# Moving five layer norms of a two-layer hybrid kernel from the scan stage into its last stage

## The chip, the core and the metric

The kernel runs on one core of a Trainium2 chip. The core's engines work side by side, each through its own queue in order: PE (TensorE, matrix products into PSUM), DVE (VectorE), ACT (ScalarE), POOL (GpSimd) and SP (SyncE, which here only starts DMA transfers). POOL starts DMA transfers as well. The metric is the time of one execution on the device in microseconds.

## What is computed

The input `x` is (2, 256, 64, 64): two batches of 256 channels and 4096 positions. Layer 0 is a group norm and a selective scan (Mamba) over the positions, added to `x`. Layer 1 is two of these, forward and backward, behind two layer norms, and then an expert layer on the layer norm of the result. The part that the change touches is the last line:

```python
t = t + _L1_ffn_ref(_ln_t(t), Wr, br, W1, ..., Wo, bo)

def _L1_ffn_ref(x, Wr, br, W1, b1, g1, be1, m1, v1, W2, b2, g2, be2, m2, v2, Wo, bo):
    feat = jnp.mean(x, axis=0)
    w = jax.nn.softmax(feat @ Wr + br, axis=-1)
    h = jnp.einsum('bfd,edh->bfeh', x, W1) + b1
    h = jax.nn.relu(_bn(h, g1, be1, m1, v1))
    h = jnp.einsum('bfeh,ehk->bfek', h, W2) + b2
    h = jax.nn.relu(_bn(h, g2, be2, m2, v2))
    y = jnp.einsum('bfeh,ehd->bfed', h, Wo) + bo
    return jnp.einsum('bfed,fe->bfd', y, w)
```

All eight experts run on every token. The weights `w` of a position are the softmax of logits that are taken from the mean over both batches, so the routes of a position need the norm of both batches there.

## The kernel before

The 4096 positions are cut into 8 chunks of 512 (`T`). A tile of a chunk holds the 256 channels as 2 x 128 partitions, [128, 2, 512] in float32, 512 KB. There are 16 such tiles, one for each batch and chunk, and 128 expert pairs: a pair here is one expert on one batch and chunk.

**The scan stage** runs six jobs one after the other, three for each batch (layer 0, forward, backward), each over 8 chunks. The backward job goes through the chunks from 7 to 0. The main loop (lines 1014 to 1058) walks over half quads, called slots; in each it issues the scans and what a table `sl` has planned for that slot and queue, and `in_order` then fixes the order on every engine. ACT makes the decays (`da`, line 664), POOL the inputs `bq` (line 654) and a part of the products with C (line 715), DVE the scans (line 690) and the rest of the products (line 699), PE the sums over states (line 723) and all projections.

**Features and early experts.** When the backward job has finished a chunk, `finish` (line 744) stores the result in `t_dram` and calls `features` (line 781, called at line 779): mean on PE, subtraction `fcen` on DVE, squares on ACT, variance on PE, the inverse root on ACT, the product on DVE and a store to `nf_dram`. This is the experts' layer norm. The last chunk of the last job is left out (`i + 1 < len(steps)`). A tile that has its features stands in `featured` and in `ready`, and the planner `experts` (line 847) puts its expert pairs into slots of the scan stage as far as its bounds for PE (`PE_ROOM`), ACT (`ACT_ROOM`) and PSUM banks allow; chunks come in the order in which they are ready. Its results `u` go to DRAM (`store`, line 940). It places 80 of the 128 pairs: all of batch 0, and chunks 7 and 6 of batch 1. Those planned beyond the last scan run in a drain (`sl.run_all` at line 1061).

**The last stage** (from line 1065) takes the other 48 pairs: chunks 5, 4, 3, 2, 1, 0 of batch 1. `rest` lists the chunks with pairs left, sorted by the number of early pairs; `whole` lists the two chunks, 7 and 6, that have none left. A pair is `layer` twice (products `hp`, line 1208, and ReLU, line 1212), `weigh` (the product with its route weights `wb`, line 1219, on DVE) and, three pairs later, `last_layer` (products into `y`, line 1227). With it goes side work, one function call at a time:

- the routes of a chunk: `load_n` (POOL starts the loads of the normed tiles, line 1093), `layer_norm` (lines 1095 to 1111, only for a tile without features), `both` (the sum `nm` of both batches on POOL, line 1115), `logits` (PE, line 1122, then six small operations on DVE and one on ACT), `spread` (transposes on PE, line 1147, a store to DRAM, and the load of `wb`, 2 MB, which repeats the weights over the partitions);
- the sums of a chunk: `load_x` (SP), `bias` (PE line 1170, ACT line 1171, and `x` plus bias on POOL, line 1173), `add_early` for each early pair (SP loads `u`, DVE multiplies by `wb`, line 1178, and adds to `x`, line 1179), and `store` (SP, line 1182).

The list `side[i]` holds what goes beside chunk i: first all sums of the whole chunk before, then the routes of the next chunks interleaved with the sums of chunk i. After each pair an equal part of what is left is issued (lines 1289 to 1293). Buffers that matter: `u` has three (the squares of `layer_norm` use the same tag), `n` six, `x` six, `wb` two.

Of the kernel before, what the change touches and what calls it, by code (L numbers as in the profile page):

```python
# [42 lines left out]
F32 = mybir.dt.float32  # L43
# [4 lines left out]
P = 128  # L48
NB, C, L = 2, 256, 4096
KC = C // P  # L50
T = 512
# [24 lines left out]
        out=(16, 18),  # L76
    ),
}
FIRST = -60
E = 8  # L80

# [50 lines left out]
def hybrid_kernel(ctx: ExitStack, tc: tile.TileContext, a: dict, out: bass.AP):  # L132
# [43 lines left out]
    early, u_dram, featured = {}, {}, set()  # L176
# [9 lines left out]
    with ExitStack() as st:  # L186
# [557 lines left out]
        def finish(i):  # L744
            (job, c), ck, tag = steps[i], cks[i], tags[i]
            s, b = job.cols(c), job.batch
            v = {}

            def load():
                v["x"] = wk.tile([P, KC, T], F32, tag="xr", name=f"xr_{tag}")  # L750
                src = t_dram[b] if job.layer else a["x"][b].rearrange("(k p) l -> p k l", p=P)
                nc.sync.dma_start(v["x"], src[:, :, s])

            def over_time(m):
                return v["x"][:, m, ::-1] if job.flip else v["x"][:, m, :]

            def project(m):
                v[m] = psp.tile([P, T], F32, tag="ps", name=f"o_{tag}_{m}")
                nc.tensor.matmul(v[m], ident, over_time(m), start=True, stop=False)
                for j in range(job.nj):  # L760
                    nc.tensor.matmul(  # L761
                        v[m], job.w["out"][:, j, m * P : (m + 1) * P], ck["sz", j],
                        start=False, stop=(j == job.nj - 1),
                    )

            s0 = starts[i + 1]

            before = steps[i - 1][0].nj if i else 0
            sl.put(max(s0 - (10 if job.nj == 4 else 5), starts[i] + (21 if before == 4 else 0)), "sp", load)

            slots = SLOTS[job.nj]["out"] if i + 1 < len(steps) else (3, 4)
            for slot in slots:
                sl.count(s0 + slot, 1 + job.nj, 1, (1,))
            for m, slot in enumerate(slots):
                sl.put(s0 + slot, "pe", lambda m=m: project(m))
                sl.put(s0 + slot + 1, "act", lambda m=m: nc.scalar.copy(over_time(m), v[m]))
            sl.put(s0 + slot + 2, "sp", lambda: nc.sync.dma_start(t_dram[b][:, :, s], v["x"]))
            if job.flip and i + 1 < len(steps):
                features(b, NCH - 1 - c, v, s0 + slot + 2)

        def features(b, c, v, s0):
# [231 lines left out]
        done = []  # L1013
# [51 lines left out]
    with ExitStack() as st:  # L1065
# [17 lines left out]
        def load_n(i):  # L1083

            if (0, i) in n:
                return
            for b in range(NB):
                n[b, i] = mk.tile([P, KC, T], F32, tag="n", name=f"n_{i}{b}", bufs=6)
                if (b, i) in featured:
                    src = nf_dram[b][:, i, :, :]  # L1090
                else:
                    src = t_dram[b][:, :, i * T : (i + 1) * T]
                nc.gpsimd.dma_start(n[b, i], src)

        def layer_norm(i):
            for b in range(NB):
                if (b, i) in featured:
                    continue
                v = n[b, i]
                mean = psp.tile([P, T], F32, tag="ps", name=f"mean_m{i}{b}")  # L1100
                for k in range(KC):
                    nc.tensor.matmul(mean, mean_w, v[:, k, :], start=(k == 0), stop=(k == KC - 1))
                nc.vector.tensor_tensor(v, v, over_channels(mean), ALU.subtract)
                sq = mk.tile([P, KC, T], F32, tag="u", name=f"sq_{i}{b}", bufs=3)
                nc.scalar.activation(sq, v, AF.Square)
                var = psp.tile([P, T], F32, tag="ps", name=f"var_m{i}{b}")
                for k in range(KC):
                    nc.tensor.matmul(var, mean_w, sq[:, k, :], start=(k == 0), stop=(k == KC - 1))
                r = mk.tile([P, T], F32, tag="r", name=f"r_{i}{b}", bufs=1)
                rsqrt(r, var, eps5)  # L1110
                nc.vector.tensor_tensor(v, v, over_channels(r), ALU.mult)

        def both(i):
            n["sum", i] = mk.tile([P, KC, T], F32, tag="nm", name=f"nm_{i}", bufs=1)
            nc.gpsimd.tensor_tensor(n["sum", i], n[0, i], n[1, i], ALU.add)

        def logits(i):

            lt = psp.tile([P, q, E], F32, tag="ps", name=f"lt_{i}")
            for t in range(q):  # L1120
                for k in range(KC):
                    nc.tensor.matmul(
                        lt[:, t, :], n["sum", i][:, k, t * P : (t + 1) * P], wr[:, k, :],
                        start=(k == 0), stop=(k == KC - 1),
                    )
            w = n["w", i] = mk.tile([P, q, E], F32, tag="w", name=f"w_{i}")
            nc.vector.tensor_tensor(
                w, lt, br.rearrange("p (o e) -> p o e", o=1).to_broadcast([P, q, E]), ALU.add
            )
            mx = mk.tile([P, q], F32, tag="mx", name=f"mx_{i}")  # L1130
            nc.vector.tensor_reduce(mx, w, AX.X, ALU.max)

            def over_experts(v):
                return v.rearrange("p (q o) -> p q o", o=1).to_broadcast([P, q, E])

            nc.vector.tensor_tensor(w, w, over_experts(mx), ALU.subtract)
            nc.scalar.activation(w, w, AF.Exp)
            sm = mk.tile([P, q], F32, tag="sm", name=f"sm_{i}")
            nc.vector.tensor_reduce(sm, w, AX.X, ALU.add)
            nc.vector.reciprocal(sm, sm)  # L1140
            nc.vector.tensor_tensor(w, w, over_experts(sm), ALU.mult)

        def spread(i):

            pt = psp.tile([P, T], F32, tag="ps", name=f"wt_{i}")
            for t in range(q):
                nc.tensor.transpose(pt[:E, t * P : (t + 1) * P], n["w", i][:, t, :], ident)
            wts[i] = mk.tile([E, T], F32, tag="wt", name=f"wts_{i}", bufs=3)
            nc.scalar.copy(wts[i], pt[:E, :])
            w_dram = drp.tile([E, T], F32, name=f"w_dram{i}")  # L1150
            nc.gpsimd.dma_start(w_dram, wts[i])
            wb[i] = mk.tile([P, E, T], F32, tag="wb", name=f"wb_{i}")
            nc.gpsimd.dma_start(
                wb[i], w_dram.rearrange("e (o t) -> o e t", o=1).to_broadcast([P, E, T])
            )

        def routes(i):
            return [lambda: load_n(i), lambda: layer_norm(i), lambda: both(i), lambda: logits(i), lambda: spread(i)]

        def load_x(i):  # L1160
            for b in range(NB):
# [76 lines left out]
            (b, i, e) for i in rest  # L1238
            for e in (order if i == rest[0] else range(E)) for b in range(NB) if e >= first[b, i]
        ]  # L1240
        side = {i: [] for i in rest}
        for at, i in enumerate(rest):
            after = rest[at + 1 : at + 2]
            now, work = sums(i), side[i]
            if at:
                for j in whole[at - 1 : at]:
                    work += sums(j)
            ahead = []
            for j in whole[at : at + 1] + after:
                ahead += routes(j)  # L1250
            every = max(1, len(now) // max(1, len(ahead)))
            while now or ahead:
                work += ahead[:1] + now[:every]
                ahead, now = ahead[1:], now[every:]

        load_n(rest[0])
        for name, e in [("W1", order[0]), ("W2", order[0]), ("W1", order[1]), ("W2", order[1])]:
            load_w(name, e)
        nc.sync.dma_start(bo, a["bo"])
        layer_norm(rest[0])  # L1260
        both(rest[0])
        for i in whole[:1] + rest[1:2]:
# [9 lines left out]
        for at, (b, i, e) in enumerate(pairs):  # L1272
            for name, k in weights[: 6 if at else 4]:
                load_w(name, k)
            weights = weights[6 if at else 4 :]
            h = layer(n[b, i], 0, e, f"{i}_{e}_{b}")
            h = layer(h, 1, e, f"{i}_{e}_{b}")
            if at == 0:
                logits(i)
            elif at == 1:  # L1280
                spread(i)

            for p in {0: [], 1: [], 2: waiting[:1], 3: waiting[1:]}.get(at, waiting[-1:]):
                weigh(*p)
            waiting.append((b, i, e, h))
            if len(waiting) > 3:
                last_layer(*waiting.pop(0))
            done[i] += 1
            work = side[i] if at > 1 else []
            upto = -(-len(work) // (count[i] - done[i] + 1))  # L1290
            for fn in work[:upto]:
                fn()
            side[i] = side[i][upto:]
        weigh(*waiting[-1])
        for p in waiting:
            last_layer(*p)
# [104 lines left out]
```

## Time and profile before

| what | us |
|---|---|
| median of three runs (5131.54 to 5132.48) | 5132.12 |
| the profiled execution | 5134.52 |
| its span, first to last instruction | 5132.7 |
| scan stage, end of the last scan's work on DVE | 4507.9 |
| last product of an early expert on PE | 4529.94 |
| first product of the last stage on PE | 4543.67 |
| end of the last product on PE | 5127.16 |

Busy time over the whole span: PE 4283.0 us (83%), DVE 4581.7 (89%), ACT 3681.3 (72%), POOL 4410.3 (86%). These are averages over two stages with different limits. In the page's row of 40 slices DVE and POOL stand at 9 tenths through nearly all of the scan stage and fall to 3 to 6 and to 1 or 0 in the last slices, where PE stands at 8 or 9. So each stage is to be read by itself.

The profile's rows have the form: start, duration, engine, line, operation, output and inputs with the kernel's names, and in brackets the idle time before it with what ended it. "PEld" is the load of a matrix into the array, which overlaps PE. A queue with a small q (SPq) means the sequencer that issues. A matrix product of the program in float32 shows as two passes.

### The profile page before, as it was taken

To read this page: it belongs to the slowest core of one execution; us is meant where nothing else is said; L and a number is where in the kernel's file an instruction comes from. 1 tells how busy PE (TensorE), PEld (TensorE's weight loads), DVE (VectorE), ACT (ScalarE), POOL (GpSimd) and SP (SyncE) were. 2 spreads that over 40 slices of the span, in tenths; PEclk is the share of its full clock that TensorE was granted. 3 is DMA by queue.
4 is the path that set the end of the run, shared out by engine and by line. 5 is a ranking of instruction groups with operands and counts; after the bars stand their busy time and mean duration, and the time that the engine had idled before them with its cause. 6 is when DMAs were issued, how large, how long until landed. Compare 5 with 4: busy or idle time off the path is not lost.

```text
span 5132.7 us, 47350 instructions
## 1 busy us (share of the span) xinstructions
PE 4283.0 (83%) x14920; PEld 1485.7 (29%) x14920; DVE 4581.7 (89%) x3088; ACT 3681.3 (72%) x7474; POOL 4410.3 (86%) x1442
## 2 busy tenths in 40 slices
PE   5677767776668988888988888899999999888999
PEld 1222222221122323333322233233333333333444
DVE  6998999999999999999989999999999999936543
ACT  5777677777767888888888788888778878832232
POOL 5998999999999999999989999999999999911100
PEclk8888888887888999999999999999999999999999
DMA  5454433344444454546654555455554444455532
GB/s 178 149 176 158 164 136 128 132 146 144 151 139 156 170 195 163 184 165 209 207 185 170 174 181 179 159 167 177 195 187 166 167 165 161 168 180 182 191 108 77
DMA packets 321355, 845.49 MB, mean 165 GB/s; under 512 B 35720, under 2 KB 107152, under 8 KB 279120
## 3 DMA queue, kind: packets, MB, share of 16 engines
q1 hardware_dynamic: 316816, 815.07, 46.2%
q0 software_dynamic: 4288, 27.40, 1.4%
q8 instruction: 118, 1.93, 0.2%
q14 instruction: 133, 1.09, 0.1%
HBM read 655.05 MB, written 187.30 MB: 164 GB/s over the span
## 4 chain that ended last, share of the span: by engine, by line
DVE 20%; PE 15%; ACT 10%; issue 4%; POOL 3%; DMA 2%; SPq 0%; DVEq 0%; POOLq 0%; ACTq 0%
DVE da L690 9%; PE hp L1208 5%; DVE bq L699 5%; ACT da L664 4%; PE y L1227 2%; PE e L912 2%; DVE bq L690 2%; POOL bq L654 2%; PE conv L452 1%; POOL bq L715 1%; PE y L723 1%; ACT bq L675 1%; DVE x L1179 1%; DVE u L1178 1%; ACT eh L923 1%
## 5 line engine op out<-in xcount | busy, mean ns | idle before, releaser
L654 POOL TENSOR_TENSOR bq<-rxdt,bc 128x2048 f32<-128x2048 f32 x640 | 2893.2, 4543 | 28.7 <-issue 12.3
L664 ACT ACTIVATE da<-rdt,w_a 128x512 f32<-128x512 f32 x2560 | 1756.8, 686 | 105.4 <-DVE bq L690 59.8
L690 DVE TENSOR_TENSOR_SCAN da<-da,h_state,bq 128x1024 f32<-128x1024 f32 x664 | 1559.1, 2348 | 50.5 <-ACT da L664 34.4
L715 POOL TENSOR_TENSOR bq<-bq,bc 128x2048 f32<-128x2048 f32 (+1 forms) x280 | 1179.9, 4214 | 22.5
L690 DVE TENSOR_TENSOR_SCAN bq<-da,h_state,bq 128x1024 f32<-128x1024 f32 x456 | 1059.3, 2338 | 28.5 <-ACT da L664 28.4
L723 PE MATMUL y<-bq,stack 128*32 128x512 f32 x5120 | 759.4, 687 | 317.4 <-POOL bq L715 297.3
L699 DVE TENSOR_TENSOR bq<-da,bc 128x1024 f32<-128x1024 f32 x760 | 926.5, 1219 | 16.0
L912 PE MATMUL e<-eh,ew 128*128 128x512 f32 x1280 | 626.1, 620 | 66.0 <-DVE sp L513 15.0
L709 ACT COPY h_state<-da 128x2 f32<-128x2 f32 x759 | 119.1, 157 | 641.3 <-DVE bq L699 639.4
L675 ACT ACTIVATE bq<-h_state,bq,a 128x1 f32<-128x1 f32 x1120 | 430.5, 384 | 0.6
L723 PEld LDWEIGHTS y<-bq,stack 128*32 128x32 f32 x5120 | 143.6, 119 | 876.7 <-POOL bq L715 404.9
L1212 ACT ACTIVATE h<-hp,of,sc 128x512 f32<-128x512 f32 x192 | 149.1, 777 | 298.9 <-PE hp L1208 281.7
L912 PEld LDWEIGHTS e<-eh,ew 128*128 128x128 f32 x1280 | 230.3, 193 | 452.0 <-issue 219.4
L414 PE MATMUL xs<-nx,w_in 128*128 128x512 f32 x640 | 318.7, 628 | 40.9 <-DVE xc L466 20.8
L452 PE MATMUL conv<-xs,w_conv 64*64 64x512 f32 x2560 | 332.6, 613 | 21.9 <-ACT xs L436 18.9
L414 PE MATMUL z<-nx,w_in 128*128 128x512 f32 x640 | 323.8, 639 | 18.7 <-DVE sp L513 10.6
L912 PE MATMUL e<-en,ew 128*128 128x512 f32 x640 | 308.3, 613 | 23.9 <-DVE fcen L809 7.8
L761 PE MATMUL o<-sz,w_out 128*128 128x512 f32 x640 | 301.7, 612 | 0.0
L923 ACT ACTIVATE eh<-e,of,sc 128x512 f32<-128x512 f32 x320 | 242.1, 768 | 36.7 <-PE e L912 36.2
L517 POOL TENSOR_TENSOR xdt<-sp,xc 128x512 f32<-128x512 f32 x160 | 203.2, 1273 | 49.9 <-DVE sp L513 49.8
L730 PE MATMUL y<-xc,w_d 128*128 128x512 f32 x320 | 193.1, 688 | 54.2 <-DVE sz L742 53.9
L690 DVE TENSOR_TENSOR_SCAN da<-da,bq 128x1024 f32<-128x1024 f32 x96 | 219.4, 2286 | 6.5 <-ACT da L664 3.6
(139 smaller groups left out, 4940.5 us busy)
## 6 DMA issues: line engine op xcount, KB each, us to landing
rxdt<-xdtd SPq DMA_DIRECT2D x160, 1024.0 KB, 6.8
rdt<-dtd SPq DMA_DIRECT2D x160, 1024.0 KB, 6.5
bc<-bcd SPq DMA_DIRECT2D x384, 256.0 KB, 3.2
dtd<-sp SPq DMA_DIRECT2D x160, 256.0 KB, 3.5
xdtd<-xdt SPq DMA_DIRECT2D x160, 256.0 KB, 4.0
ew<-in_W SPq DMA_DIRECT2D x160, 256.0 KB, 4.3
u<-u SPq DMA_DIRECT2D x80, 512.0 KB, 4.4
u<-eu SPq DMA_DIRECT2D x76, 512.0 KB, 4.0
```

What stands on the lines that cost most here:

```text
L414: nc.tensor.matmul(ps, job.w["in", half][:, k, j * P : (j + 1) * P], rhs, start=(k == 0), stop=(k == KC - 1),)
L452: nc.tensor.matmul(v[r][64 * col : 64 * col + 64, :], job.w["conv"][rows, 2 * jp + j, k, :], ck["xs", jp][rows, j, k : k + T] if k < 4 els ...
L654: nc.gpsimd.tensor_tensor(bq[g], ck["rxdt", j], over_groups(ck["bc", 0, sg]), ALU.mult)
L664: nc.scalar.activation(da[g, h][:, k, :], cks[i]["rdt", j][:, q, :], AF.Exp, scale=steps[i][0].w["a"][:, j, q * SG + sg : q * SG + sg + 1],)
L675: nc.scalar.activation(bq[g][:, q, 0:1], job.h[:, j, sg, q : q + 1], AF.Identity, scale=cks[i]["a0", j][:, h, sg : sg + 1], bias=bq[g][:, ...
L690: nc.vector.tensor_tensor_scan(b if on_pool(g, h) else d, d, b, job.h[:, j, sg, 2 * h : 2 * h + 1] if c else 0.0, ALU.mult, ALU.add,)
L699: nc.vector.tensor_tensor(bq[g][:, two, :], d, cks[i]["bc", 1, sg].rearrange("p (o t) -> p o t", o=1).to_broadcast([P, 2, T]), ALU.mult,)
L715: nc.gpsimd.tensor_tensor(b, b, cks[i]["bc", 1, sg].rearrange("p (o t) -> p o t", o=1).to_broadcast([P, groups, T]), ALU.mult,)
L723: nc.tensor.matmul(y[i, j][q * CG : (q + 1) * CG, :], stack, bq[g][:, q, :], start=False, stop=(sg == SG - 1),)
L761: nc.tensor.matmul(v[m], job.w["out"][:, j, m * P : (m + 1) * P], ck["sz", j], start=False, stop=(j == job.nj - 1),)
L912: nc.tensor.matmul(ps, ew[l][:, k, m * P : (m + 1) * P], key[x][:, k, :], start=(k == 0), stop=(k == KC - 1),)
L923: nc.scalar.activation(key[dst][:, m, :], key["ps", l, m], AF.Relu, bias=of[:, l, e, m : m + 1], scale=sc[:, l, e, m : m + 1],)
```

## The change

Five tiles of batch 1, those of chunks 4, 3, 2, 1 and 0, no longer get their features in the scan stage: `AHEAD = 3` lets only the first three chunks of the last job have them. (Chunk 0 had none before either.) Their norm is made in the last stage. There the norm is cut in two functions: `centred` (mean, subtraction, squares) and `layer_norm` (variance, inverse root, product), which are two entries in the list of routes; the squares have a tag and a buffer of their own.

With four feature norms fewer, the planner places 82 pairs early: experts 0 and 1 of batch 1's chunk 5 come in addition. Since chunk 5 then has more early pairs than the others, `rest` becomes 4, 3, 2, 1, 0, 5. Chunk 4 is the first, and both halves of its norm are issued ahead of the first pair.

The side work now has fixed places. Every entry has a share of the chunk's pairs, and is issued as soon as the share of pairs done is greater: the six parts of the routes at 0, 0.15, 0.25, 0.4, 0.6 and 0.8 (a second chunk's 0.1 later each), and the sums evenly from 0.1 on, those of the whole chunk before first.

```diff
+AHEAD = 3
...
-            if job.flip and i + 1 < len(steps):
+
+            if job.flip and (b < NB - 1 or c < AHEAD):
                 features(b, NCH - 1 - c, v, s0 + slot + 2)
...
-        def layer_norm(i):
+        def centred(i):
             for b in range(NB):
                 if (b, i) in featured:
                     continue
...
                 nc.vector.tensor_tensor(v, v, over_channels(mean), ALU.subtract)
-                sq = mk.tile([P, KC, T], F32, tag="u", name=f"sq_{i}{b}", bufs=3)
+                sq = n["sq", b, i] = mk.tile([P, KC, T], F32, tag="sq", name=f"sq_{i}{b}", bufs=1)
                 nc.scalar.activation(sq, v, AF.Square)
+
+        def layer_norm(i):
+            for b in range(NB):
+                if (b, i) in featured:
+                    continue
+                v, sq = n[b, i], n["sq", b, i]
                 var = psp.tile([P, T], F32, tag="ps", name=f"var_m{i}{b}")
...
-            return [lambda: load_n(i), lambda: layer_norm(i), lambda: both(i), lambda: logits(i), lambda: spread(i)]
+            return [lambda: load_n(i), lambda: centred(i), lambda: layer_norm(i), lambda: both(i), lambda: logits(i), lambda: spread(i)]
...
-        side = {i: [] for i in rest}
+        side = {}
         for at, i in enumerate(rest):
-            after = rest[at + 1 : at + 2]
-            now, work = sums(i), side[i]
+            side[i] = []
+            for k, j in enumerate(whole[at : at + 1] + rest[at + 1 : at + 2]):
+                for part, fn in zip((0, 0.15, 0.25, 0.4, 0.6, 0.8), routes(j)):
+                    side[i].append((part + 0.1 * k, fn))
+            now = sums(i)
             if at:
-                for j in whole[at - 1 : at]:
-                    work += sums(j)
-            ahead = []
-            for j in whole[at : at + 1] + after:
-                ahead += routes(j)
-            every = max(1, len(now) // max(1, len(ahead)))
-            while now or ahead:
-                work += ahead[:1] + now[:every]
-                ahead, now = ahead[1:], now[every:]
+                now = [fn for j in whole[at - 1 : at] for fn in sums(j)] + now
+            side[i] += [(0.1 + 0.9 * k / len(now), fn) for k, fn in enumerate(now)]
+            side[i].sort(key=lambda work: work[0])
...
         nc.sync.dma_start(bo, a["bo"])
+        centred(rest[0])
         layer_norm(rest[0])
         both(rest[0])
...
-            work = side[i] if at > 1 else []
-            upto = -(-len(work) // (count[i] - done[i] + 1))
-            for fn in work[:upto]:
-                fn()
-            side[i] = side[i][upto:]
+            while at > 1 and side[i] and (done[i] == count[i] or side[i][0][0] < done[i] / count[i]):
+                side[i].pop(0)[1]()
```

## The prediction, made before the changed kernel was run

> **What bounds the kernel now.** I read four views in this order: the busy times by window, the chain of waits over the last 600 us, the timeline at the seam between the scans and the experts' stage, and the timeline around the one norm that the last stage already holds.
>
> The windows are cut at the chunks of the last job's scans (the first product of line 730 of each chunk), then at the first expert product of each chunk in the last stage. Columns: length, then busy time of PE, PEld, DVE, ACT and POOL.
>
> ```profile
> 3643.60:3752.60 109.00, 102.36 (x373) 35.89 (x372) 103.09 (x67) 83.63 (x160) 108.44 (x35) 0.97 0.53 185
> 3972.00:4082.50 110.50, 99.97 (x366) 34.95 (x365) 107.03 (x70) 88.56 (x186) 107.39 (x35) 0.97 0.51 175
> 4191.90:4302.60 110.70, 99.96 (x366) 33.88 (x365) 106.98 (x70) 88.93 (x186) 107.43 (x35) 0.95 0.50 169
> ...
> 4507.20:4543.70 36.50, 22.77 (x53) 9.58 (x53) 0.68 (x1) 6.62 (x10) 2.35 (x5) 0.87 0.38 134
> 4628.90:4741.90 113.00, 97.25 (x242) 43.61 (x241) 70.29 (x65) 28.74 (x40) 19.17 (x14) 0.92 0.55 198
> 4741.90:4844.30 102.40, 97.23 (x223) 42.25 (x222) 74.11 (x65) 27.79 (x38) 14.72 (x9) 0.93 0.56 195
> 4844.30:4933.20 88.90, 88.82 (x218) 38.49 (x217) 35.15 (x35) 27.42 (x37) 11.41 (x11) 1.00 0.40 143
> ```
>
> To see: in the scans DVE and POOL are both at 97% and more, and the first chunk shown, which holds no feature norm, is 1.5 us shorter than the other two: there POOL alone is full. In the last stage PE is the bound where nothing goes wrong (88.82 of 88.90), and the second and third chunk lose time. The chain of waits names the cause:
>
> ```profile
> 4693.13 1.15 DVE u L1178
> 4694.30 1.24 DVE x L1179
> 4695.99 5.06 DMA x<-t_dram
> 4701.19 1.18 POOL x L1173
> 4703.49 2.33 POOL x L1173
> 4705.82 3.29 POOL nm L1115
> 4709.15 3.59 PE lt L1122 x16
> ```
>
> The sums of a whole chunk come as one block on DVE; SP's next load stands behind the store of that block, POOL's sum `nm` behind that load, PE's logits behind `nm`: 12.4 us of idle PE. Seam and norm:
>
> ```profile
> 4530.85 0.53 POOL L942 DMA_DIRECT2D u<-eu  x1 [6.61 <-ACT eu L921]
> 4543.67 5.75 PE L1208 MATMUL hp<-n,W 128*128 128x512 f32 x8 [13.73 <-DMA W<-in_W]
> ...
> 4956.37 1.98 PE L1102 MATMUL mean_m<-n,mean_w 128*128 128x512 f32 x4
> 4958.39 1.22 DVE L1103 TENSOR_TENSOR n<-n,mean_m 128x1024 f32<-128x1024 f32 x1 [15.80 <-PE mean_m L1102]
> 4959.65 1.06 ACT L1105 ACTIVATE sq<-n 128x1024 f32<-128x1024 f32 x1 [2.58 <-DVE n L1103]
> 4960.76 3.68 PE L1108 MATMUL var_m<-sq,mean_w 128*128 128x512 f32 x4 [2.40 <-ACT sq L1105]
> 4964.48 0.69 ACT L179 ACTIVATE r<-var_m,columns 128x512 f32<-128x512 f32 x1 [2.47 <-PE var_m L1108]
> 4965.18 1.28 ACT L180 ACT_TABLE_LOAD   x1
> 4966.48 0.63 ACT L180 ACTIVATE r<-r 128x512 f32<-128x512 f32 x1
> ```
>
> To see: the stage starts 13.73 us after the last early expert, on DMA; and a norm with nothing between its steps makes PE idle 2.4 us and then run four passes in 3.68 instead of 1.98 us.
>
> **What the Trainium skill says.** "SBUF — State Buffer", section "SBUF: two separate sides": DVE with two SBUF inputs and POOL hold one shared port pair exclusively. The trace agrees: three `h` products took 6.42 us (2.14 each, else 1.22) beside `nm`, which took 3.32 us instead of 2.34; the subtraction from PSUM at 4958.39 took 1.22 us beside POOL. "TensorE: Matmul & The Clock Gate", "What's actually happening": an idle window of about 3.4 us puts the array at half clock. Here 2.4 us were enough, costing 1.7 us. "ScalarE: Activation LUTs", "What ACT_TABLE_LOAD costs": 1283 ns and a drain of 1380 ns; the trace has 1.28 us and the next activation 0.02 us later, so I use 1.28.
>
> **The change, part by part.** Each Matmult of the program is two passes of 0.43 us (eight passes, 3.43 us in the chain), so an expert pair of 12 costs PE 10.57 us (spacing of `hp` starts in clean pairs).
>
> (1) Scans. The features of four chunks leave: per chunk 4 products, 2 DVE passes of 1.2 us (line 809: 1.21), 4 short ACT passes, a store on SP. By the changed order each of these chunks gets 4 early-expert products for them, so PE stays. DVE loses 2.4 us per chunk. POOL's own floor is some 107.3 us plus 0.6 idle. The chunk without features took 109.0 against 110.3 for the mean of four with them and 36 expert products (110.5, 110.5, 109.4, 110.7): I take 1.5 us x 4 = -6. Bounds: 0 (POOL is the whole limit, or PE) and -9.7 (all DVE time counts).
>
> (2) Drain. After the last scan's sum PE has 38 products instead of 26 ahead of the seam, nothing else runs: 12 x 0.87 = +10.4. The two new pairs 5/0 and 5/1 of the second batch end there; their store gates the seam as pair 6/7's did.
>
> (3) Seam. Chunk 4 becomes first, because chunk 5 has two early pairs; its second-batch tile comes from `t_dram` rather than `nf_dram`. The same source took 9.1 us against 8.4 (medians to landing in the stretch 4900 to 4960): +0.5. Bounds 0 and 1.
>
> (4) First norm, exposed: mean on a cold array 3.7, subtraction 1.25, square 1.1, variance 3.7, logarithm 0.7, table 1.3, exponential 0.65, product 1.3, between them 0.1: +13.8. No pair can hide it, since all need that tile or come later in PE's queue. Bounds 12 and 15.
>
> (5) Pairs: 46 instead of 48, 2 x 10.57 = -21.1.
>
> (6) Norms beside pairs: four instead of one, each 8 passes: 3 x 3.86 = +11.6.
>
> (7) Stalls. Before: 48 x 10.57, 8 logits of 1.70, 8 transposes of 0.44, 8 biases of 1.92 and a norm of 3.86 make 543.7; from 4543.67 to 5127.16 are 583.5, so 39.8 stall. After, worked out from the order:
> - 2.1 cold start, as before.
> - Chunk 3's two halves run in one turn (fractions 0.25 and 0.35, both under 3/8): mean and variance stand together on PE. Ahead of the subtraction DVE waits for `wb` of chunk 4, 12.5 us after its transposes ended (wts copy, 3.5 and 7.5 us to landing); PE is ready 11 us after them. With the slowed product (2.1), subtraction and square the variance is 6.0 late, and cold: 7.7. Bounds 5 and 10.
> - Chunk 2's halves stand together too. Ahead of the subtraction DVE has four of chunk 7's sums, which start 5.05 us after the bias product (4754.32 to 4759.34) and share the port with two POOL passes. Some 15 us from there to the square, PE ready after 9 (one pair less the bias): 6.6 and the cold clock, 8.3. Bounds 4 and 12.
> - Chunk 1's halves are a pair apart, so only its mean can be late: the load of its tile on POOL stands behind the load of `wb` of chunk 2, which waits until DVE has finished with chunk 3. I put the landing 5 us after PE wants it: 6.8 with the cold clock. Bounds 0 and 12.
> - Chunk 0's halves are apart, its loads early: nothing. Table loads sit under PE's products as at 4960.72; with the rest I allow 1.5.
> Together 26.4, so -13.4. The old 12.4 us stall goes because `nm` of chunks 7, 6, 3, 2 and 1 now stands ahead of the late bias sums on POOL.
>
> Steps that cost nothing: the extra 512 KB buffer frees `u`; `mean`, `var` and the table loads on ACT find PE's next products running (ACT is busy 28 of 102 us there); the 10 sums of chunk 5 have six pairs to hide in. If DVE is late, none of this cover holds.
>
> Sum: -6 + 10.4 + 0.5 + 13.8 - 21.1 + 11.6 - 13.4 = -4.2. The profiled execution took 5134.5 with a span of 5132.7, 2.4 over the median of the runs; the difference applied to the median gives 5127.9.
>
> **Rivals.** (A) Forecast: 5127.9, chance 0.42.
> (B) Faster: the norms hide better. Scans give 9 instead of 6, chunk 1's tile is in time (-6.8), chunk 2's subtraction is 2 us earlier: -16 in all, 5116. For it: DVE runs ahead in clean chunks (35 of 89 us busy). Against it: chunks 3 and 2 each carry 24 sums of 2.39 us, 9 products and 5 or 6 POOL passes on the shared port, about 100 us with the waits behind stores. Chance 0.27.
> (C) Scans give nothing, since POOL is their limit: +1.8, 5133.9. For it: POOL 107.4 in every chunk; against it the 109.0 us chunk. Chance 0.10.
> (D) Slower: DVE becomes the bound of chunks 3 and 2. Each store of a finished chunk holds up SP's next loads: before, 5.34, 6.97, 7.03 and 5.87 us of idle DVE, and 13.9 at 4747 where the loads met that of `wb` (I used 5.3 and 7). In the new order loads and a `wb` may meet at two seams; with 13.9 at both, DVE is 13.8 us later. Its logits of chunk 1 have only some 3.5 us before PE's transposes want them: beyond that point each microsecond stalls PE. 10 us there, 3 each at the norms of chunks 3 and 2: +16, so +11.8 and 5143.9. For it: DVE and PE need nearly the same time in these chunks. Against it: each PE stall also gives DVE time back. Chance 0.21.
>
> **How the numbers follow.** About 0.2% (10.3 us) is what a measurement tells from no change. A and C lie within it: 0.52; B is faster: 0.27; D slower: 0.21. B and D at their own values need most of the range: 5114 to 5144 leaves some 2 in 10 outside. A alone spans 5121 to 5136.
>
> **What would show it.** Step 1: chunks 4 to 6 of the last job at 108.5 to 109.5 us. Steps 2 to 4: the first `hp` some 29 us later relative to the last scan. Step 7: gaps of 6 us before `var_m` of chunks 3 and 2, a wait of `mean_m` of chunk 1 for a DMA, none before `lt`. I am wrong if PE waits at `wt` or `lt` for DVE or POOL (D), if `mean_m` of chunk 1 does not wait (B), or if the norm ahead of the first pair is hidden.

## The result, and the profile after

The changed kernel takes 5153.83 us (median of 6 runs, 5151.49 to 5155.26) beside 5131.83 us before (5128.81 to 5133.11): a ratio of 1.0043, 95% interval 1.0033 to 1.0053. It is slower by 22 us. The profiled execution took 5155.26 us with a span of 5153.4, 20.7 more than the span before.

Busy times by window, kernel after. The columns are those of the table in the prediction; the numbers after the last parentheses are the mean granted clock of PE, the DMA share and the DMA's GB/s. The first row is the scans of the last job's last four chunks, the second runs from the last scan's sum on PE to the start of the experts' stage, the third is the first norm, the others are the second to fourth chunk of the last stage.

```profile
4081.00:4494.60 413.60, 382.77 (x1370) 133.96 (x1368) 399.63 (x249) 333.84 (x692) 400.79 (x128) 0.97 0.49 168
...
4494.60:4544.00 49.40, 34.79 (x77) 14.84 (x77) 0.69 (x1) 10.90 (x16) 2.84 (x5) 0.85 0.37 122
4544.00:4558.10 14.10, 7.57 (x9) 2.35 (x9) 2.44 (x2) 4.94 (x5) 0.01 (x1) 0.50 1.07 360
4654.10:4777.10 123.00, 105.62 (x250) 45.71 (x249) 77.97 (x70) 33.46 (x45) 20.09 (x14) 0.89 0.47 163
4777.10:4891.00 113.90, 97.35 (x230) 41.59 (x229) 71.95 (x63) 33.08 (x44) 16.28 (x13) 0.93 0.54 194
4891.00:4983.40 92.40, 92.33 (x225) 39.89 (x224) 39.90 (x38) 31.46 (x41) 9.13 (x7) 1.00 0.37 130
```

The same four chunks before, in the same view:

```profile
4082.50:4507.20 424.70, 386.57 (x1378) 136.96 (x1377) 408.71 (x258) 340.65 (x704) 401.00 (x128) 0.97 0.48 164
```

The scans gained 11.1 us. POOL did the same work (401.00 and 400.79 us), DVE 9.1 us less, ACT 6.8 and PE 3.8 less. So the stretch got shorter by 2 us more than DVE lost, with POOL busy 94% of it before and 97% after. Counted between the first products of line 731, the three chunks that were to take 108.5 to 109.5 us took 107.3, 109.1 and 105.8. In the last stage the chunk without a whole chunk's sums (last row) is as tight as before, 92.33 busy of 92.40. The second and third chunk lose: 123.0 and 113.9 us, with 17 us of idle PE each and a clock of 0.89 and 0.93.

What PE waits for from 4530 us to the end, kernel after. The numbers are us in total, times, longest.

```profile
PE hp L1216 <- ACT h L1220: 26.0, 2, 16.5
PE var_m L1116 <- ACT sq L1107: 14.9, 3, 7.8
PE mean_m L1104 <- DMA n<-t_dram: 14.6, 1, 14.6
PE hp L1216 <- DVE n L1119: 4.0, 1, 4.0
```

The last two rows and 2.6 us of the second are the seam and the first norm, 4.5 and 7.8 of the second row the norms of chunks 3 and 2. The seam and the three norms were forecast. The first row was not: the second layer of a pair waits twice for the ReLU of its first layer, a step of 0.8 us on an engine that is busy 33 of 114 us there. The timeline at the longer of the two, on PE, DVE and ACT:

```profile
4835.56 1.85 PE L1130 MATMUL lt<-wr,nm 128*128 128x8 f32 x16
...
4837.26 3.68 PE L1216 MATMUL hp<-n,W 128*128 128x512 f32 x8
...
4837.84 1.23 DVE L1186 TENSOR_TENSOR u<-u,wb 128x1024 f32<-128x1024 f32 x1 [4.16 <-DMA u<-u]
...
4854.67 1.23 DVE L1187 TENSOR_TENSOR x<-x,u 128x1024 f32<-128x1024 f32 x1
4855.81 0.18 DVE L1135 TENSOR_TENSOR w<-lt,br 128x32 f32<-128x32 f32 x1
4856.03 0.19 DVE L1139 TENSOR_REDUCE mx<-w 128x4 f32<-128x32 f32 x1
4856.25 0.19 DVE L1144 TENSOR_TENSOR w<-w,mx 128x32 f32<-128x32 f32 x1
4856.48 0.23 ACT L1145 ACTIVATE w<-w 128x32 f32<-128x32 f32 x1 [23.37 <-DVE w L1144]
4856.61 1.43 ACT L1220 ACTIVATE h<-hp,of,sc 128x512 f32<-128x512 f32 x2
...
4857.43 6.65 PE L1216 MATMUL hp<-h,W 128*128 128x512 f32 x8 [16.48 <-ACT h L1220]
```

PE has the logits `lt` ready at 4837.4. DVE reaches them at 4855.8, because fourteen operations of whole-chunk sums and one `h` product (1.2 us each) stand before them in its queue. The exponential of the logits (L1145) is ACT's and was issued with the logits, so it stands in ACT's queue ahead of the next pair's ReLUs and holds them for 16 to 17 us; PE stands still and then runs eight products in 6.65 instead of 3.87 us, which the same eight take elsewhere in this kernel. The other stop, 9.5 us, is behind the logits of chunk 6, beside chunk 3. "Perfetto Trace Analysis", section "Tensor Engine Instruction (MATMUL, LD_WEIGHTS)", of the Trainium skill says that ACT and DVE are strictly first in, first out. The trace agrees: two ReLUs whose products had ended by 4840.9 start 0.13 us after that exponential starts. DVE is late without being full: in the second chunk's 123.0 us it is busy 78.0, and ahead of the first stop it waits there 13.9 us for `wb`, 11.7 for POOL's sum of `x` and bias, and 8.1 for loads of `u`.

### The profile page after: what moved, and what is told of

It reads as the page before. It is cut to its first block, busy times and chain, and to the rows that moved or that the text cites. A ratio compares the mean times of both kernels' runs of the same rounds, so it can differ in the third digit from the quotient of the medians.

```text
span 5153.4 us, 47366 instructions
## 1 busy us (share of the span) xinstructions
PE 4285.9 (83%) x14920; PEld 1483.4 (29%) x14920; DVE 4591.5 (89%) x3090; ACT 3691.3 (72%) x7480; POOL 4411.4 (86%) x1443
## 4 chain that ended last, share of the span: by engine, by line
DVE 25%; PE 19%; ACT 12%; POOL 6%; issue 6%; DMA 2%; SPq 0%; DVEq 0%; POOLq 0%; ACTq 0%
DVE da L691 12%; DVE bq L700 6%; ACT da L665 5%; PE hp L1216 5%; POOL bq L655 4%; PE e L914 3%; DVE bq L691 3%; PE y L1235 3%; POOL bq L716 2%; PE conv L453 2%; PE y L724 2%; ACT bq L676 1%; PE o L762 1%; ACT eh L925 1%; DMA dtd<-sp 1%
## 5 line engine op out<-in xcount | busy, mean ns | idle before, releaser
L914 PE MATMUL e<-eh,ew 128*128 128x512 f32 x1312 | 641.2, 620 | 56.4 <-DVE sp L514 14.1
L453 PE MATMUL conv<-xs,w_conv 64*64 64x512 f32 x2560 | 331.3, 610 | 20.9 <-ACT xs L437 19.0
```

The lines of the kernel that those rows point to most:

```text
L453: nc.tensor.matmul(v[r][64 * col : 64 * col + 64, :], job.w["conv"][rows, 2 * jp + j, k, :], ck["xs", jp][rows, j, k : k + T] if k < 4 els ...
L914: nc.tensor.matmul(ps, ew[l][:, k, m * P : (m + 1) * P], key[x][:, k, :], start=(k == 0), stop=(k == KC - 1),)
```

## The experiments

The theory: **the queue**. DVE runs late on the sums of a whole chunk; an ACT operation that needs DVE's result then stands in ACT's queue ahead of ReLUs that do not need it, and PE stops. The rivals: the moved norms themselves take the time, or DVE and the port it shares with POOL are full, so that a wait that is taken away comes back elsewhere. Whether quicker loads of `u` would also have kept DVE in time was not tried. Each median is set against the runs of the kernel before in the same comparison.

**Only the fixed shares.** The norms stay in the scan stage, 80 early pairs, the new side work.

```diff
-AHEAD = 3
+AHEAD = 7
```

> The features back in the scan stage (AHEAD = 7, so 80 early pairs, first chunk 5, one norm left in the last stage), with the fixed shares kept. Theory Q (queue): the vector queue runs late on the sums of chunks 7 and 6, the exponential of the logits waits for it in ACT's queue, and the ReLUs behind it stop PE. The two whole chunks' sums are then beside chunks 4 and 3 just as they are beside 3 and 2 in the changed kernel, so two waits of hp for ACT of 8 to 17 us stay, no others over 3 us: 5120 to 5135 us. Theory N (norms): the five norms in the last stage make the loss and make DVE late; without them the waits go and the fixed shares show their gain over before, whose last stage holds some 36 us of stalls: 5095 to 5110 us.

Measured: 5145.78 us, ratio 1.0025 (1.0015 to 1.0036). PE's waits in the last stage:

```profile
PE hp L1216 <- ACT h L1220: 42.6, 2, 21.8
PE hp L1216 <- DMA n<-nf_dram: 12.6, 1, 12.6
```

With no norm moved, the wait for the ReLU is there, and longer than in the changed kernel. The fixed shares alone cost some 13 us. The time is above both expected ranges: the two waits were 21.8 and 20.9 us where the theory of the queue had 8 to 17.

**Only the moved norms.** `AHEAD = 3`, the old distribution of the side work:

```diff
-                for part, fn in zip((0, 0.15, 0.25, 0.4, 0.6, 0.8), routes(j)):
-                    side[i].append((part + 0.1 * k, fn))
...
+            every = max(1, len(now) // max(1, len(ahead)))
+            while now or ahead:
+                work += ahead[:1] + now[:every]
```

> The norms in the last stage as in the changed kernel, but the side work spread as before (sums of the whole chunk as a block first, then routes and sums interleaved). Theory Q: as the block came first before too, DVE is late again when the logits come; PE waits behind ACT or at POOL's nm for 20 to 40 us, and each norm has its halves in the same turn or the next; 5150 to 5175 us. Theory N: the loss is the norms, the distribution does not matter: within 5 us of the changed kernel, 5149 to 5159 us. If the fixed shares are the loss (theory S), this kernel is at 5120 to 5130 us, as the scan stage's gain of 12 us remains.

Measured: 5161.89 us, ratio 1.0055 (1.0040 to 1.0070), the slowest of all. There is no long wait for a ReLU. PE waits 16.3 us for squares, 10.0 for `nm` on POOL before the logits, 7.5 before the transposes, 5.4 for a tile. So the norms and the fixed shares are not two costs to be added: alone they cost some 29 and 13 us, together 22.

**The exponential one pair later.** The logits' function is cut behind DVE's subtraction of the maximum, and its rest (`soft`: exponential, sum, reciprocal, product) becomes a part of its own. Nothing else moves.

```diff
+        def soft(i):
+            w = n["w", i]
...
-                for part, fn in zip((0, 0.15, 0.25, 0.4, 0.6, 0.8), routes(j)):
+                for part, fn in zip((0, 0.15, 0.25, 0.4, 0.6, 0.7, 0.8), routes(j)):
```

> The changed kernel with the logits cut in two: products, bias, maximum and subtraction where they were, the exponential on ACT and what follows on DVE at a share 0.1 later (one pair). The same work on every engine. Theory Q: the waits of 9.5 and 16.5 us of hp for ACT fall by one pair's time of 10.6 us each, to 0 and about 6, and the cold passes behind the first go: 5153.8 - 20 - 3 = 5131 us, range 5126 to 5138. Rival L (load): DVE and the shared port are the bound of these chunks, so the wait comes back at the transposes wt or at the next norm, and the time stays at 5147 to 5155 us.

Measured: 5133.66 us, ratio 1.0003 (0.9995 to 1.0012), 20.2 us under the changed kernel. PE's waits:

```profile
PE var_m L1116 <- ACT sq L1107: 14.9, 3, 7.8
PE mean_m L1104 <- DMA Wo<-in_Wo: 14.3, 1, 14.3
PE mean_m L1104 <- DMA n<-t_dram: 9.4, 1, 9.4
PE hp L1223 <- DVE n L1119: 4.0, 1, 4.0
PE hp L1223 <- DVE w L1135: 2.4, 1, 2.4
PE hp L1223 <- ACT h L1227: 0.4, 1, 0.4
```

The 26.0 us are gone, the rows of squares are untouched, and the wait for the tile of chunk 1, which the prediction had priced at 6.8 and the changed kernel did not show, appears with 9.4: PE had simply been too late to meet it. So the place in the queue of one operation of 0.23 us, with three small ones of DVE that follow it, is worth 20 us. That shows the queue as the cause of the 26.0 us. Of DVE's lateness a wait of 2.4 us for `lt` is left.

**The other whole chunk's sums later.** Chunk 6's sums go from beside chunk 2 to beside chunk 1, and its routes from beside chunk 3 to beside chunk 2; the exponential stays early.

```diff
-            for k, j in enumerate(whole[at : at + 1] + rest[at + 1 : at + 2]):
+            for k, j in enumerate((whole[at // 2 : at // 2 + 1] if at % 2 == 0 else []) + rest[at + 1 : at + 2]):
...
-            if at:
-                now = [fn for j in whole[at - 1 : at] for fn in sums(j)] + now
+            if at % 2:
+                now = [fn for j in whole[at // 2 : at // 2 + 1] for fn in sums(j)] + now
```

> The changed kernel with the routes of chunk 6 beside chunk 2 and its 16 sums beside chunk 1 instead of chunk 2. Theories Q and L: chunk 2 then has 8 sums instead of 24, DVE is in time for its logits and the wait of 16.5 us with its 2.8 us of cold passes goes; beside chunk 1 DVE is late in turn, as a chunk with 24 sums, and one wait of 5 to 17 us appears there at the logits of chunk 0. Time 5140 to 5154 us. If the lateness came from the norm of chunk 1 standing in DVE's queue ahead of the sums (theory N), the chunk without sums loses nothing and chunk 1, whose norm partner is chunk 0, loses as much: no change, 5150 to 5156, and the same wait moves with the norm. A wait at the logits of chunk 3's second route (9.5 us) stays under both.

Measured: 5149.55 us, ratio 1.0034 (1.0021 to 1.0048); the intervals overlap with those of the changed kernel. PE's waits for ReLUs:

```profile
PE hp L1216 <- ACT h L1220: 33.4, 2, 16.8
```

A wait stays in chunk 3, now behind the logits of chunk 2 and longer than expected (16.6 us, 9.5 in the changed kernel), and the other moves with the sums to chunk 1 (16.8 us at 4945.7). One whole chunk beside one chunk is enough to make DVE late; two in a row aren't needed.

**Seven norms ahead and the late exponential**, the edits of the first and third run together:

```diff
-AHEAD = 3
+AHEAD = 7
```

> Features back in the scan stage (AHEAD = 7) together with the late exponential of x_exp_late; with x_ahead7, x_exp_late and the changed kernel it makes a square. Theory Q: the two waits of 21.8 and 20.9 us lose 10.6 us each, and some more where DVE no longer waits for ACT: 5145.8 - 22 = 5124 us (5119 to 5129), so the norms' move costs some 8 to 10 us with either order of the exponential (5153.8 - 5145.8 = 8; 5133.7 - 5124 = 10). Theory N (norms make DVE late, and the exponential only shows it): the move costs nothing once the exponential is late, 5130 to 5137 us.

Measured: 5124.48 us, ratio 0.9982 (0.9975 to 0.9989). The ReLU's wait is gone, and PE waits 21.6 us in another way:

```profile
PE hp L1223 <- DVE w L1135: 21.6, 2, 13.3
```

DVE's lateness now reaches PE through PSUM, where `hp` and `lt` share one set of buffers: a product of the first layer needs one that still holds logits which DVE has not read, and starts 0.24 us after DVE starts to read them. The four runs make a square: moving the norms costs 8.0 us with the early exponential (5153.8 against 5145.8) and 9.2 with the late one (5133.7 against 5124.5).

**Three repairs of the norms**, each on top of the one before, the late exponential in all: the norm's second half a pair after the first; then chunk 5, which has its features, as first chunk of the stage, so that no norm stands ahead of it; then a third buffer for `wb`.

```diff
-                for part, fn in zip((0, 0.15, 0.25, 0.4, 0.6, 0.7, 0.8), routes(j)):
+                for part, fn in zip((0, 0.15, 0.3, 0.4, 0.6, 0.7, 0.8), routes(j)):
...
-        rest.sort(key=lambda i: sum(first[b, i] for b in range(NB)))
+        rest.sort(key=lambda i: (any((b, i) not in featured for b in range(NB)), sum(first[b, i] for b in range(NB))))
...
-            wb[i] = mk.tile([P, E, T], F32, tag="wb", name=f"wb_{i}")
+            wb[i] = mk.tile([P, E, T], F32, tag="wb", name=f"wb_{i}", bufs=3)
```

> x_exp_late with the second half of a norm at share 0.3 instead of 0.25, so that a pair stands between the halves for chunks 3 and 2 as well. The waits of var_m of 4.5 and 7.8 us and 1.8 us of cold passes at each go: -15 of waits if nothing takes their place, 5119 us. Theory L (DVE is the bound of chunks 3 and 2): the variance is in time, but DVE gets no more time, and the wait is passed on to the logits' exponential or to the tile of chunk 1, which already makes PE wait 9.4 us: 5125 to 5134 us. I expect half of it to be passed on: 5126 us.

> x_apart with chunk 5 first again (six pairs, its tiles have features), so that chunk 4's norm is beside pairs. The norm ahead of the first pair, 14.1 us from the first mean product to the first hp, goes from PE's idle time: -10.2 (14.1 less 3.9 of work that stays) against x_apart if its halves are hidden. Rival: chunk 5 has only six pairs to hide the routes of 7 and 4 and its 10 sums, so DVE or POOL's loads are late by the first pairs of chunk 4: gain below 4 us.

> x_first5 with three buffers for wb instead of two. POOL then need not wait for DVE's last product of a chunk before it loads the next wb and the tiles behind it in its queue. If the 9.4 us wait of mean_m for a tile from t_dram is due to that block, it goes, with 1.8 us of cold passes: -8 to -11 us against x_first5. If it is due to the transfers all running at once, or to the n buffers, it stays: within 3 us.

Measured: 5129.90 (ratio 0.9995, 0.9986 to 1.0004), 5131.89 (0.9999, 0.9990 to 1.0007) and 5124.60 us (0.9983, 0.9975 to 0.9992). The first takes away the 12.3 us at the norms of chunks 3 and 2, and 6.8 us for ReLUs and 4.8 for the logits' buffer come back (0.4 and 2.4 before it). The second takes away the first norm's exposed chain, and a wait of 11.4 us for the squares of chunk 4 takes its place, since nothing of the side work is issued before the stage's third pair, so that both halves of that norm fall into one turn there while DVE waits for `wb`: a miss. Neither of the two is told apart from the run with the late exponential (the intervals overlap). The third is 9.1 us below that run; it takes away the late tile of chunk 1 (7.2 us in the run before it): the load of that tile stands on POOL's queue behind a `wb` load which waits for a buffer, as step 7 had said.

**The whole chunks' sums spread.** On top of the late exponential, the norm's second half at 0.3 and chunk 5 first: half of chunk 7's sums goes beside each of the second and third chunks, half of chunk 6's beside each of the fourth and fifth, with a buffer of their own for their weights and other shares for the routes beside the first chunk; then the same with seven norms ahead.

```diff
+            for j in whole[(at - 1) // 2 : (at - 1) // 2 + 1] if at else []:
+                of_j = sums_of.setdefault(j, sums(j))
+                now += of_j[:11] if at % 2 else of_j[11:]
+            now += sums(i)
```

> The changed kernel with the logits' exponential one pair later, the last job's featured chunk 5 first in the last stage, the second half of a norm at 0.3 of a chunk's products, and the sums of the two whole chunks no longer each beside one chunk: half of chunk 7's sums beside each of the second and third chunks of the stage, half of chunk 6's beside each of the fourth and fifth, with a buffer of their own for the whole chunks' weights. Theory (VectorE is late only because a whole chunk's sums fall beside one chunk, and every wait left in the stage follows from that lateness): the waits of the same kernel with whole sums and three buffers, 11.1 us (chunk 4's norm), 5.1 (the ReLU) and 8.8 (a logits buffer not read), go, and with them some 5 us of products that restart slowly: 5124.6 - 25 - 5 = about 5095, taken as 5093 to 5106. Rival (VectorE and the port that it shares with GpSimd are full in the whole stage, so that evened work only moves the waits): 5118 to 5128, with waits of over 15 us in all spread over more chunks.

> The same as the run with evened sums, but with the norms of all seven chunks ahead of the last stage, as in the kernel before, and the exponential one pair later. Theory of lateness: the two waits of 8.3 and 13.3 us for a logits buffer in the run with seven norms ahead and the late exponential go, some 3 us of slow restarts with them: 5124.5 - 24.6 = about 5100, taken as 5096 to 5107. If moving the norms costs some 8 to 9 us on top in every variant, as in the two pairs of runs so far, this is 8 us under the run with three norms ahead; if evened sums give VectorE room for the norms, the two lie within 4 us. Rival (VectorE full): 5118 to 5128.

Measured: 5110.36 us (ratio 0.9962, 0.9947 to 0.9977) and 5107.23 us (0.9951, 0.9934 to 0.9968). From 4600 us on PE is busy throughout in both but for 1.5 us, so DVE isn't full: it was late only where a whole chunk's sums fell beside one chunk. The first kernel misses its expected range by some 4 us (the second by 0.2), for a wait of 13.4 us at the beginning of the stage:

```profile
4572.36 1.98 PE L1104 MATMUL mean_m<-n,mean_w 128*128 128x512 f32 x4
...
4576.92 1.95 DVE L1235 TENSOR_TENSOR h<-h,wb 128x1024 f32<-128x1024 f32 x1 [19.47 <-DMA wb<-w_dram]
...
4588.19 1.21 DVE L1105 TENSOR_TENSOR n<-n,mean_m 128x1024 f32<-128x1024 f32 x1
...
4589.43 1.06 ACT L1107 ACTIVATE sq<-n 128x1024 f32<-128x1024 f32 x1 [16.38 <-DVE n L1105]
4590.40 1.43 ACT L1228 ACTIVATE h<-hp,of,sc 128x512 f32<-128x512 f32 x2
```

It is the same queue with other names: the squares of a norm wait for DVE's subtraction, which stands behind sums, and the ReLUs stand behind the squares. With three norms ahead or with seven, the two times can't be told apart any more (the intervals overlap).

**That norm's first half earlier**, ahead of the stage's first weighing, where DVE stands idle for 19.5 us (its old place in the list is left out):

```diff
             elif at == 1:
                 spread(i)
+            elif at == 2:
+                centred(rest[1])
```

> The run with evened sums and three norms ahead, with one step moved: the first half of the second chunk's norm comes one pair earlier, ahead of the first weighing of the stage, where VectorE still waits for the first chunk's weights (19.5 us idle there). Theory (the 13.4 us for a ReLU in that run is the same queue again: the Square of chunk 4's norm stands in ScalarE's queue before the ReLUs of the next pair, and waits for VectorE's subtraction, which stands behind the sums that had piled up): the 13.4 us go, and the 2.6 us of a product that restarts slowly: 5110.4 - 16 = 5094, taken as 5091 to 5100. Then moving the norms into the stage gains beside seven norms ahead with the same evened sums (5107.2). Rival (VectorE has no room, the wait only moves to the norm's second half or to the logits): 5106 to 5112 with a wait of 8 us or more at another place.

Measured: 5109.09 us, ratio 0.9953 (0.9940 to 0.9967): not told apart from the run before, and 9 us above the expected range. The 13.4 us are gone and a wait of the logits for `nm` has come:

```profile
PE lt L1130 <- POOL nm L1123: 6.0, 1, 6.0
```

But PE, busy without a gap from 4605 us on, ends hardly earlier, because it runs slower. PE's timeline at one of four like places:

```profile
4767.94 3.60 PE L1243 MATMUL y<-h,Wo 128*128 128x512 f32 x8
4771.47 1.98 PE L1185 MATMUL bi<-wts,bo 8*128 8x512 f32 x4
4773.38 3.18 PE L1130 MATMUL lt<-wr,nm 128*128 128x8 f32 x16
4776.41 5.80 PE L1224 MATMUL hp<-n,W 128*128 128x512 f32 x8
```

No gap stands between these rows, and yet the logits take 3.18 instead of 1.95 us and the products 5.80 instead of 3.68. What precedes is the product with the bias, which uses 8 rows of the array, and then logits 8 columns wide.

**The bias product one pair earlier** from the second chunk on, with the load of `x` for it, so that full products stand between it and the logits:

```diff
-            side[i] += [(0.1 + 0.9 * k / len(now), fn) for k, fn in enumerate(now)]
...
+            late = len(now) + 1
...
+            for k, fn in enumerate(now):
+                side[i].append((0.1 + 0.9 * k / len(now) - (0.13 if at and k in (late - 1, late) else 0), fn))
```

> The run with the norm's first half early, with one step moved: from the second chunk of the stage on, the product with the bias (four passes over 8 rows, 1.98 us) comes one pair earlier, so that a pair's full products stand between it and the 16 short products of the logits (1.95 us). In the run before, and in the one with evened sums and seven norms ahead, the two stand next to each other four times, and after each the granted clock is 0.6 to 0.7 for some 5 us though TensorE waits for nothing (5.38 to 6.19 us for eight products that else take 3.68). Theory (3.9 us of such thin products in a row let the clock fall): the four slow stretches go, 10.1 us in that run's profile: 5109.1 - 10.1 = 5099, taken as 5095 to 5104. Rival (the clock falls for another reason, such as the long stretch without a pause): 5106 to 5112, with as much of the slow clock at other places.

Measured: 5101.35 us, ratio 0.9941 (0.9928 to 0.9955), the fastest of all; its profiled span is 5100.1 us against 5107.2. The intervals of the two ratios overlap, so the verdict rests on the trace: from the stage's first product to its last 551.2 us against 561.0, where the four slow stretches had cost 10.1. The windows of the last stage, the run before first (clock: third number from the end):

```profile
4640.00:4740.00 100.00, 99.92 (x238) 42.90 (x238) 68.54 (x58) 33.58 (x45) 18.14 (x12) 0.98 0.47 163
4740.00:4840.00 100.00, 99.93 (x249) 44.54 (x248) 46.24 (x48) 32.96 (x45) 13.41 (x11) 0.97 0.47 163
```

```profile
4640.00:4740.00 100.00, 99.92 (x242) 42.83 (x241) 70.52 (x58) 33.40 (x44) 19.66 (x12) 1.00 0.47 163
4740.00:4840.00 100.00, 99.90 (x257) 43.84 (x256) 52.06 (x48) 34.93 (x47) 16.11 (x11) 1.00 0.48 163
```

PE is busy for the same time in both and issues more products in the second, at a clock of 1.00. None of the four slow stretches is left.

## Why the prediction was wrong

The forecast was 5127.9 us, within 5114 to 5144; the kernel took 5153.83. By its own steps, in the profiled executions:

| step | forecast | measured | from |
|---|---|---|---|
| 1 scans | -6 | -12.6 | last scan's sum on PE ends at 4494.60, before 4507.15 |
| 2 drain | +10.4 | +12.0 | 34.8 us of PE work after it, before 22.8 |
| 3 seam | +0.5 | +0.9 | 14.60 and 13.73 us |
| 4 first norm | +13.8 | +14.1 | 4543.99 to 4558.06 |
| 5 pairs | -21.1 | -21.1 | counted, not measured by itself |
| 6 norms beside pairs | +11.6 | +11.6 | counted, as above |
| 7 stalls | -13.4 | +16.4 | 590.4 us of stage less 534.2 of work is 56.2; before 39.8 |
| sum | -4.2 | +21.3 | end of the last product 5127.16 and 5148.43 |

Steps 2, 3 and 4 held within 1.6 us. (The sign "some 29 us later" for the first `hp` doesn't follow from them: they add up to 24.7, and 26.9 were measured.) Step 1 had the right sign and too small a size: it took POOL as the floor because it was busy 97% of each chunk, and allowed 1.5 us a chunk. Of the 12.6 us, 1.5 were there before the first of the four chunks; the other 11.1 (2.1, 1.6, 4.7 and 2.7 by chunk) still go beyond its bound of -9.7. Its floor of 107.9 us a chunk (107.3 of POOL's work, 0.6 idle) did not hold: the shortest of the first three chunks took 105.8.

Step 7 failed by 29.8 us. Its named parts were right for two of three: the norms of chunks 3 and 2 cost 6.3 and 9.6 us with the slow clock, where 7.7 and 8.3 were set down; the tile of chunk 1, 6.8, did not show, because PE came too late to wait for it. What failed is the term "with the rest I allow 1.5". The paragraph of steps that cost nothing let ACT's `mean`, `var` and table loads "find PE's next products running", and the exponential of the logits, which stands in the same queue, was given no price at all. Two exponentials held up the ReLUs: 26.0 us of wait and 5.5 of slow restarts, 31.5 together. The rest of the stall is 8.8 us, where 2.1 and 1.5 were allowed: 2.5 at the cold start, 0.8 behind chunk 2's norm, 3.4 where a bias product follows logits (last section), and some 2 that stay open.

Rival D came closest to it. It named the place of the second stop (DVE late on the sums of chunks 3 and 2, at the logits of chunk 1) but the wrong point from which it decides: it asked when PE's transposes want the weights, which is more than a pair after the logits, and allowed 10 us there. ACT's queue wants them before the next ReLU. With that consumer the lateness of DVE, 11 and 18 us from the end of the logits to DVE's first operation on them, goes into PE nearly whole: 9.5 and 16.5. The sentence "If DVE is late, none of this cover holds" was in the prediction and was not carried into a number. The signs that were to show D, waits at `wt` or `lt`, did not appear, because the stop came earlier in the chain. The sign of B, no wait of `mean_m` of chunk 1, did appear, and not for B's reason: the norms did not hide better, PE was late.

What the change could bring is a separate matter. Taking the norms out of the scans cost 8.0 and 9.2 us where the side work was uneven; with even side work the two are not told apart. The kernel of 5101.35 us has the moved norms, but the last two repairs weren't tried with seven norms ahead, so no gain of the move itself is shown. An estimate speaks against one: the slow stretches of the even kernel with seven norms ahead add up to 11.7 us in its trace, and without them its 5107.2 would be some 5095 us. The gain beside both kernels comes from the order of the side work.

## What to carry to other kernels

Where a stage's operations are placed by hand, list for each engine what stands behind every operation that waits for another engine: the price of a late result is set by the first unrelated work behind its first consumer, not by the last consumer that needs it. Spread a block of side work before tuning single places, and put half a chain whose other half is late one step later. After a wait has gone, compare the granted clock and the length of single products as well as the gaps.

## What was not expected of the hardware

**PE slowed without a pause.** The Trainium skill, "TensorE: Matmul & The Clock Gate", section "What's actually happening", ties the clock to how busy the array was in a free-running window of 3413 ns and tells of idle windows. Here the bias product (1.98 us, 8 rows) and, right behind it, the logits (1.95 us, 8 columns), 3.9 us with no gap on PE, were followed by slow products (5.38 to 6.19 us for eight, else 3.68) at four places of four in two kernels (with the norm's half early, and with seven norms ahead and even sums), and at one of four in the even one with three ahead. At the place whose timeline stands among the experiments (4773.3 to 4782.2 us) the granted clock was 0.62. With the logits first, three of the six places that no long wait cuts in two were slow, one of them in the changed kernel, where PE had run at full speed again after its stop of 9.5 us:

```profile
4747.95 1.85 PE L1130 MATMUL lt<-wr,nm 128*128 128x8 f32 x16
4749.73 2.80 PE L1178 MATMUL bi<-wts,bo 8*128 8x512 f32 x4
4752.46 6.23 PE L1216 MATMUL hp<-n,W 128*128 128x512 f32 x8
```

Where full products stood between the two, no place was slow unless PE had just waited. A free-running window fits the uneven counts; it isn't shown. One place costs 1.7 to 3.4 us. The prediction's reading that 2.4 us of idle time were enough for the slow clock is open to the same cause: there, too, a bias product had ended only 2 us before the idle time, and 1.46 us of idle time between full products (at 4579.97 us, seven norms ahead with the early exponential) slowed nothing.

**POOL at 94% was not the limit.** In the last four chunks of the scans POOL kept its 401 us of work, and the stretch still became 11.1 us shorter: POOL's idle time fell from 23.7 to 12.8 us. DVE's work fell by 9.1 us and stayed at 96 to 97% of the stretch. That DVE had been the limit is the likely reading and isn't shown, since ACT and PE had less to do as well.
